# Row biases of a graph network: added by GpSimd and VectorE in place of a bf16 product on TensorE

## The chip, the cores and the metric

The kernel runs on one core of a Trainium2 chip. Its engines are TensorE (called PE in the profile, with PEld for the loading of its stationary operand), VectorE (DVE), ScalarE (ACT), GpSimd (POOL) and SyncE (SP), which only issues transfers here. The metric is the device time of one execution in microseconds (us).

## The reference, cut to what matters

Four layers of a graph network act on `x`, 512 rows of 768 numbers. Each layer normalizes `x`, gives it to a graph part and to a mixer, adds both to `x`, normalizes again and adds a feed-forward part. What matters here are the biases that are one row long, that is, one number per column, the same for all 512 rows:

```python
# layer 0, graph part, at its end: attention
qkv = nodes @ Wqkv.T + bqkv
...
attended = attn @ Wo.T + bo
return nodes + attended
# layer 0, mixer: values with a bias, and a projection with a bias
qkv = x @ qkv_w.T + qkv_b
...
out = out @ proj_w.T + proj_b
# layer 1, mixer: projection with a bias, then gamma, beta and a norm
# layers 2 and 3, mixers
out = out @ w_proj + b_proj
```

The kernel knows them as seven rows: `m0_bv` and `g0_bv` (the third of the qkv biases that belongs to the values, of mixer 0 and of the attention of graph part 0), `g0_bo` (that attention's output), and `m0_bp`, `m1_bp`, `m2_bp`, `m3_bp` (the projections of mixers 0 to 3). All matrix products are in float32, and the biases have to arrive in float32 precision too.

## The kernel before, in words

The 512 rows are `NT` = 4 tiles of `P` = 128 partitions, the 768 columns are `KC` = 6 chunks of 128 for a contraction, or two halves of `HW` = 384 for an output. The residual `self.x` ([128, 4, 768]) stays in SBUF for the whole program. Weights are streamed by SP in blocks of 1152 KB into a ring of six buffers, in the order in which the program uses them.

`tm` (L368) computes an output with rows on partitions: for each half `nb` and each row tile `t` it takes a PSUM bank, accumulates six (or twelve) products into it by `acc`, and hands the bank to `done`, which evicts it. One call is eight accumulations. `add_x` (L476) is the eviction that adds a bank to `self.x` on VectorE. `copy` (L280 and L282) is one that copies, on VectorE and ScalarE in turn.

A row bias is one more product at the end of an accumulation. `bias` (L312) fetches the row to one partition (`row`), and `parts` cuts it into three bf16 numbers that sum to the float32 value, by three copies and two subtractions on that one partition; they land at partitions 0, 32 and 64 of `self.bias3`, whose other partitions stay zero. The stationary operand is `spread(0)`, a column of `self.sel` broadcast to 128 columns, with ones at those partitions, so that a 96x128 by 96x384 product in bf16 adds the row to all 128 rows of the bank. `self.bias3` has two slots that `self.which` alternates.

The seven places, in the order of the program:

- `mix0`: the values' eight accumulations, with `m0_bv`, whose row is prepared at the program's start inside `meanwhile` by ScalarE and VectorE (all the others are prepared by GpSimd).
- `in_units`: the projection of mixer 0, cut into eight units that a generator hands out one at a time as filler inside the graph part, with `m0_bp`.
- `attention0`: its values with `g0_bv`, and `g0_wo` with `g0_bo`.
- `mix1_end`: a transfer brings `be` to 128 partitions, GpSimd adds it to `x` (L1572); then the projection with `m1_bp` is added by `put_y` onto `y`, the normalized input, which is normalized again, scaled and added to `x`.
- `project`, called by `mix2`: the projection with `m2_bp`. Mixer 2 begins with `operands` (L1861 on ScalarE, L1870 on GpSimd), which splits its input in parts, while `thirds` (L1890, L1891 on VectorE) does so with a weight.
- `last_two`: mixer 3 and the graph part of layer 3 run in alternation; each `m3_wp` accumulation has `m3_bp`, prepared behind `self.picked`.

The order on each engine is made by a list scheduler when the program is built: an engine takes, among the instructions that are ready in its model, the one that comes first in the program, so later work can move ahead of earlier work that isn't ready. `tc.issue_after(i)` adds an edge: what is issued in its block comes after `i`. At run time each engine, and the transfers that it issues, keeps its order: what stands in front and waits holds up what is behind it. GpSimd issues all the small transfers.

Of the kernel before, what the change touches and what calls it, by code (L numbers as in the profile page):

```python
# [10 lines left out]
F32 = mybir.dt.float32  # L11
# [184 lines left out]
class Net:  # L196
    def __init__(self, ctx, tc, dram, at, out):
# [28 lines left out]
        self.sel = keep.tile([96, 32], BF16, name="sel")  # L226
        self.bias3 = self.rowp.tile([96, 2, D], BF16, name="bias3", bufs=1)
        nc.gpsimd.memset(self.bias3, 0.0)
        self.which = 0

# [80 lines left out]

    def bias(self, ap, n=D, copies=None, sub=None):  # L312

        t = self.row(ap, n)
        mid = self.rowp.tile([1, D], BF16, name="mid", bufs=1)
        self.which ^= 1
        out = self.bias3[:, self.which, :n]
        self.parts(out, t[:1, :n], t[:1, :n], mid[:, :n], copies or [self.nc.gpsimd.tensor_copy] * 3,
                   sub or self.nc.gpsimd.tensor_sub)
        return out  # L320

# [45 lines left out]

    def tm(self, blocks, xT, done, bias=None, nbs=None, bias_at=0):  # L368

        for nb in range(blocks.shape[0]) if nbs is None else nbs:  # L370
            ws = [self.wk(blocks[nb, kb]) for kb in range(blocks.shape[1])]
            for t in range(NT):
                p = self.ps()
                pairs = [(xT[k][:, t * P : (t + 1) * P], ws[k // KC][:, k % KC, :]) for k in range(len(xT))]
                if bias is not None:
                    o = nb * HW - bias_at
                    pairs.append((self.spread(0), bias[:, o : o + HW]))
                self.acc(p[:, :HW], pairs)
                done(t, nb, p[:, :HW])
# [388 lines left out]
    def mix0(self, xnT, checked, held, bv):  # L768
# [3 lines left out]
        with ExitStack() as outer, ExitStack() as c:  # L772
# [12 lines left out]
            def put_v(t, nb, p):  # L785
                h = (nb - 4) * 4
                self.copy(v[:, t, h : h + 4, :96], p.rearrange("p (h d) -> p h d", h=4))

            self.tm(d["m0_wqkv"], xs, put_v, bv, nbs=(4, 5), bias_at=2 * D)
            for g in range(2):  # L790
# [64 lines left out]
    def in_units(self, aT, later, first=0):  # L855

        bias = self.bias(self.d["m0_bp"])
        for n in range(first, 8):
            nb, t = divmod(n, 4)
            if n < 2 or n % 2 == 0:  # L860
                w = self.wk(self.d["m0_wp"][nb, 0])
            p = self.ps()
            i = self.acc(p[:, :HW], [(aT[:, k, t * P : (t + 1) * P], w[:, k, :]) for k in range(KC)]
                         + [(self.spread(0), bias[:, nb * HW : (nb + 1) * HW])])
            self.add_x(t, nb, p[:, :HW])
            aT = later
            yield i.ins
# [11 lines left out]
    def project(self, c, attn, m, done=None, aT=None):  # L879

        if aT is None:
            aT = c.enter_context(self.tc.tile_pool(name=m + "_aT", bufs=1)).tile([P, KC, N], F32, name="aT")
        self.to_fm(attn, aT)
        self.tm(self.d[m + "_wp"], self.chunks(aT), done or self.add_x, self.bias(self.d[m + "_bp"]))

# [118 lines left out]
    def gnn0_any(self, nodesT, xnT, ops, EFT):  # L1004
        nc, tc, d = self.nc, self.tc, self.d
        with ExitStack() as c:
# [21 lines left out]
            with tc.tile_pool(name="g0_l", bufs=1) as lp:  # L1028
                for l in range(3):
                    h = lp.tile([P, NT, D], F32, name="h")  # L1030
                    aggT = hT = xnT
                    for f in range(KC):
                        p = self.ps()
                        self.acc(p, [(nodes[:, t, f * P : (f + 1) * P], AT[:, t, :]) for t in range(NT)])
                        nc.vector.tensor_add(aggT[:, f, :], EFP[:, f, :], p)
                    self.tm(d["g0_w1"][l], self.chunks(nodesT) + self.chunks(aggT),
                            lambda t, nb, p: self.copy(h[:, t, nb * HW : (nb + 1) * HW], p),
                            self.bias(d["g0_b1"][l : l + 1]))
# [12 lines left out]

    def attention0(self, nodesT, bv):
        nc, tc, d = self.nc, self.tc, self.d
        ns = self.chunks(nodesT)
        with ExitStack() as c:
            att = c.enter_context(tc.tile_pool(name="g0_att", bufs=1))
            two = c.enter_context(tc.tile_pool(name="g0_two", bufs=2))
            with tc.issue_after(self.after):
# [3 lines left out]
            aT = att.tile([P, KC, N], F32, name="aT")  # L1062
            self.tm(d["g0_wqkv"], ns, lambda t, nb, p: self.copy(v[:, t, (nb - 4) * HW : (nb - 3) * HW], p),
                    bv, nbs=(4, 5), bias_at=2 * D)
            for g in range(2):
# [3 lines left out]
                for h in range(4):  # L1069
# [23 lines left out]
                    else:  # L1093
                        for i in range(3):
                            self.copy(aT[96:, 3 * g + i, :], p[32 * i : 32 * i + 32])
            self.tm(d["g0_wo"], self.chunks(aT), self.add_x, self.bias(d["g0_bo"]))

    def moe(self, f, act, xn, xnT, wg, bs=None, fill=None, later=None, known=False):
# [6 lines left out]
        with ExitStack() as c:  # L1105
# [144 lines left out]
            def second_bias(t, nb):  # L1250
                p = self.ps()
                self.acc(p[:, :HW], [(gT[:, t * P : (t + 1) * P], b2[:, nb * HW : (nb + 1) * HW])])
                self.add_x(t, nb, p[:, :HW])
# [311 lines left out]
    def mix1_end(self, c, y, aT):  # L1565
# [11 lines left out]

        self.tm(d["m1_wp"], self.chunks(aT), put_y, self.bias(d["m1_bp"]))
        self.norm(y, y)
# [220 lines left out]
    def mix2(self, xnT, ops):  # L1800
        nc, tc, d = self.nc, self.tc, self.d
        xs = self.chunks(xnT)
        with ExitStack() as c:
# [27 lines left out]

            self.fm3(d["m2_wqkv"], ops, put_q, (0, 1), two)

            kv = one.tile([P, KC, P + 2], F32, name="kv")
# [233 lines left out]
    def last_two(self, xn, xnT, out, V):  # L2068
# [5 lines left out]
        with ExitStack() as c:  # L2074
# [39 lines left out]
            with tc.issue_after(self.picked):  # L2114
                bias = self.bias(d["m3_bp"])
            ready = []
            for t in range(NT):
                for nb in range(2):
                    p = self.ps()[:, :HW]
                    self.acc(p, [(qk[:, 0, k, t * P : (t + 1) * P], ws[nb][:, k, :]) for k in range(KC)]  # L2120
                             + [(self.spread(0), bias[:, nb * HW : (nb + 1) * HW])])
                    self.add_x(t, nb, p)
# [390 lines left out]
def tile_net(ctx, tc, dram, at, out, only=ALL):  # L2513
# [10 lines left out]
    with ExitStack() as ck, ExitStack() as c0:  # L2524
# [7 lines left out]
        with tc.tile_pool(name="L0", bufs=1) as pool:  # L2532
# [6 lines left out]
            def meanwhile():  # L2539
                net.constants()  # L2540
                bv.append(net.bias(net.d["m0_bv"], D, net.copies, nc.vector.tensor_sub))
                for t in range(NT):
# [9 lines left out]
            ops = net.mix0(xnT, checked, c0, bv[0])  # L2552
            bv0 = net.bias(net.d["g0_bv"])
            slot = net.which
            with tc.If(net.wrong > 0) as cmp:
                net.gnn0_any(nodesT, xnT, ops, EFT)
                net.which = 1 - slot
                net.bias(net.d["g0_bv"])
            with cmp.Else():
# [65 lines left out]
```

## Time and profile before

The time is 3710.01 us, the median of three runs (3708.91 to 3713.39). The profiled execution is another run and took 3715.96 us, with a span of 3714.2 us and a mean granted clock of TensorE of 0.992.

| | before |
|---|---|
| time, median of three runs | 3710.01 us |
| profiled execution, time and span | 3715.96 us, 3714.2 us |
| TensorE busy | 3604.8 us, 97% |
| VectorE busy | 1591.9 us, 43% |
| ScalarE busy | 892.8 us, 24% |
| GpSimd busy | 489.4 us, 13% |
| bias products (stationary `sel`, 384 columns) | 56 |
| moved from and to HBM | 714.47 MB, 192 GB/s over the span |

Times in the profile are microseconds from the span's start. A line of a timeline gives the start, the length of the group, the engine, the line of the kernel, the operation, and the tiles that it writes and reads; what stands in brackets is the idle time before it and what ended that. A line of a tile's instructions gives the count, the shortest, median and longest duration in ns, and the times between which they lie. The chain that ended last is followed back from the last instruction, at each step to what released it, or to the instruction before it on its engine; its shares say which engine's work the end had to wait for.

The feed-forward part of layer 3 fills the span from about 2605 to the end. There the weights' stream takes the DMA engines: 424 GB/s in most slices of the page, against 14 to 371 before.

### The profile page before, as it was taken

What the parts mean: (1) busy time and instruction counts of PE and PEld (TensorE: products, weight loads), DVE (VectorE), ACT (ScalarE), POOL (GpSimd) and SP (SyncE); (2) the same over time, 40 slices, a digit from 0 to 9 for tenths busy, and PEclk for the clock granted to TensorE, in tenths of its full rate; (3) what the DMA queues carried; (4) which work ended last, traced back from release to release, by engine and by line L of the source; (5) the groups of instructions that cost most, each with busy time, mean ns of one, the idle gap of its engine ahead of it and who ended that gap; (6) DMA issues with size and microseconds to landing.
All of it is one profiled execution on the core that took longest, in us unless ns stands there. A gap on an engine that the chain in (4) does not pass through costs nothing.

```text
span 3714.2 us, 39788 instructions
## 1 busy us (share of the span) xinstructions
PE 3604.8 (97%) x15741; PEld 2161.0 (58%) x15741; DVE 1591.9 (43%) x3259; ACT 892.8 (24%) x1595; POOL 489.4 (13%) x534
## 2 busy tenths in 40 slices
PE   9999999999999999999999998999999999999998
PEld 6547666445566585567878785556444444444444
DVE  8227664343212573145776764377321221221211
ACT  2223432221222263122343432254100000000000
POOL 8212101102100000010221212202000000000000
PEclk9999999999999999999999998999999999999999
DMA  5202122217501213003121114612999999999998
GB/s 214 82 14 96 58 90 102 93 44 283 199 30 56 94 57 119 26 36 112 54 76 64 64 64 184 251 51 115 371 424 423 424 424 424 424 424 424 424 425 357
DMA packets 96692, 714.47 MB, mean 192 GB/s; under 512 B 11712, under 2 KB 11968, under 8 KB 26480
## 3 DMA queue, kind: packets, MB, share of 16 engines
q1 hardware_dynamic: 75744, 604.81, 40.4%
q0 software_dynamic: 16848, 95.99, 6.8%
q10 hardware_dynamic: 3904, 11.01, 0.8%
q8 instruction: 129, 2.11, 0.2%
q14 instruction: 67, 0.55, 0.0%
HBM read 689.22 MB, written 22.54 MB: 192 GB/s over the span
## 4 chain that ended last, share of the span: by engine, by line
PE 82%; DMA 6%; issue 5%; DVE 5%; ACT 1%; POOL 0%; POOLq 0%; DVEq 0%; ACTq 0%; SPq 0%
PE ps L383 45%; PE ps L2432 12%; PE ps L1952 7%; PE ps L2448 6%; PE ps L2403 3%; PE ps L404 3%; PE ps L923 2%; DMA w<-in_f_Wg_dram 2%; DMA w<-in_f_Wu_dram 2%; PE ps L1715 2%; DMA w<-in_f_Wd_dram 1%; PE ps L1696 1%; PE ps L608 1%; DVE pt L1465 1%; DVE e L1464 1%
## 5 line engine op out<-in xcount | busy, mean ns | idle before, releaser
L2432 PE MATMUL ps<-w,xg 128*64 128x384 f32 x3072 | 565.3, 489 | 6.6 <-DMA w<-in_f_Wg_dram 3.3
L2432 PEld LDWEIGHTS ps<-w,xg 128*64 128x64 f32 x3072 | 236.8, 137 | 294.2 <-issue 262.4
L2448 PE MATMUL ps<-w,hT 128*64 128x384 f32 x1536 | 320.6, 490 | 3.3 <-DMA w<-in_f_Wd_dram 1.9
L1952 PE MATMUL ps<-ops,w 128*128 128x512 f32 x1080 | 268.0, 399 | 0.5 <-DVE w L1890 0.5
L383 PE MATMUL ps<-w,xnT 128*128 128x384 f32 x756 | 253.4, 491 | 0.2 <-ACT xnT L282 0.2
L383 PE MATMUL ps<-ops,w 128*128 128x512 f32 x972 | 242.6, 394 | 0.0
L383 PE MATMUL ps<-xnT,w 128*128 128x512 f32 x540 | 236.6, 593 | 0.1
L1952 PEld LDWEIGHTS ps<-ops,w 128*128 128x128 f32 x1080 | 204.4, 190 | 50.6 <-DVE w L1890 0.9
L2448 PEld LDWEIGHTS ps<-w,hT 128*64 128x64 f32 x1536 | 133.3, 137 | 163.2 <-issue 137.8
L2435 ACT ACTIVATE h<-ps 128x384 f32<-128x384 f32 x64 | 31.5, 492 | 794.4 <-PE ps L2432 794.4
L476 DVE TENSOR_TENSOR x<-x,ps 128x384 f32<-128x384 f32 x232 | 127.2, 553 | 199.6 <-PE ps L383 190.4
L383 PEld LDWEIGHTS ps<-ops,w 128*128 128x128 f32 x972 | 182.4, 188 | 42.5 <-issue 0.5
L383 PEld LDWEIGHTS ps<-w,xnT 128*128 128x128 f32 x756 | 144.0, 192 | 100.3 <-issue 6.8
L1861 ACT ACTIVATE w<-w 128x768 fp32r<-128x768 f32 x138 | 116.4, 847 | 331.5 <-PE ps L383 262.7
L2436 DVE TENSOR_TENSOR h<-h,ps 128x384 f32<-128x384 f32 x64 | 35.5, 554 | 354.6 <-PE ps L2432 345.9
L383 PE MATMUL ps<-w,hT 128*128 128x384 f32 x552 | 184.6, 490 | 2.9 <-ACTq L1341 1.6
L1870 POOL TENSOR_TENSOR low<-low,ops 128x512 f32<-128x512 f32 x90 | 118.5, 1317 | 432.0 <-ACT ops L1861 432.0
L383 PEld LDWEIGHTS ps<-xnT,w 128*128 128x128 f32 x540 | 101.9, 190 | 122.6 <-issue 119.3
L383 PEld LDWEIGHTS ps<-w,hT 128*128 128x128 f32 x552 | 103.1, 190 | 80.4 <-ACT xbT L282 7.1
L1890 DVE TENSOR_TENSOR w<-w,w 128x768 fp32r<-128x768 f32 x138 | 132.6, 963 | 20.4 <-ACT w L1861 20.0
L1891 DVE SCALAR_TENSOR_TENSOR w<-w 128x768 fp32r<-128x768 f32 x138 | 136.6, 992 | 2.5
L2403 PE MATMUL ps<-xnT,sw 128*128 128x512 f32 x288 | 135.4, 603 | 0.0
(566 smaller groups left out, 5155.3 us busy)
## 6 DMA issues: line engine op xcount, KB each, us to landing
w<-in_f_Wg_dram SPq DMA_DIRECT2D x128, 1152.0 KB, 22.3
w<-in_f_Wu_dram SPq DMA_DIRECT2D x128, 1152.0 KB, 22.6
w<-in_f_Wd_dram SPq DMA_DIRECT2D x128, 1152.0 KB, 22.5
w<-in_g_w_dram SPq DMA_DIRECT2D x54, 1152.0 KB, 5.1
w<-in_m_wqkv_dram SPq DMA_DIRECT2D x24, 1152.0 KB, 7.1
w<-in_g_t_dram SPq DMA_DIRECT2D x12, 1152.0 KB, 5.1
w<-in_m_wp_dram SPq DMA_DIRECT2D x11, 1152.0 KB, 5.1
ea<-in_attr_dram SPq DMA_DIRECT2D x17, 512.0 KB, 4.7
```

The costliest lines, as they stand in the source:

```text
L383: i = self.nc.tensor.matmul(out, a, b, start=n == 0, stop=n == len(pairs) - 1)
L404: return self.nc.tensor.transpose(out, in_, self.ident[:k, :k])
L476: self.nc.vector.tensor_add(xs, xs, p)
L923: nc.tensor.matmul(p, w[:, i, k], ops[:, i, k, :], start=i + k == 0, stop=i + k == KC)
L1861: return self.nc.scalar.activation(top, x, AF.Copy, scale=CUT).ins
L1870: nc.gpsimd.tensor_sub(low, v, ops[:, 0, k, :].bitcast(F32))
L1890: nc.vector.tensor_sub(low, w, top.bitcast(F32))
L1891: self.sliced_last = nc.vector.scalar_tensor_tensor(dif, low.bitcast(F32), -TIMES, top.bitcast(F32), OP.mult, OP.add).ins
L1952: nc.tensor.matmul(outs[o], w[:, i, k], ops[:, i, k, :], start=n == 0 and i + k == 0, stop=n == 4 and i + k == KC)
L2403: i = nc.tensor.matmul(p, w[:, k, :], xnT[:, k, :], start=k == 0, stop=k == KC - 1)
L2432: nc.tensor.matmul(p[a * 64 : a * 64 + 64, :HW], xg[:, k, a * CAP : (a + 1) * CAP], ws[b][a][:, k, :], start=k == 0, stop=k == KC - 1)
L2448: nc.tensor.matmul(po[nb][a * 64 : a * 64 + 64, :HW], hT[:, f * P + a * 64 : f * P + a * 64 + 64], wd[a][:, f, nb * HW : (nb + 1) * HW], s ...
```

## The change

No product for a bias is left on TensorE. A new helper, `wide`, brings a row to all 128 partitions in float32 (one buffer, so a new row waits until the last one has been read). `add_rows` does that for each of its names and then lets GpSimd add the row to the four tiles of its target, 128x768 each.

- The values of mixer 0 and of the attention are evicted by VectorE alone, by an add of the PSUM bank and the wide row, where a copy alternated between VectorE and ScalarE.
- `m0_bp` and `g0_bo` are added to `x` in `mix0`, behind `self.after` (a transfer that GpSimd issues for the edge counts), that is, long before their projections.
- `m1_bp` is added to `y` in `mix1_end` ahead of the projection, in the program behind the adds of `be`.
- `m2_bp` is added to `x` in `mix2` behind the queries' product `fm3`.
- `m3_bp` is added to `x` in `last_two`, behind `self.picked`, where the row was prepared before.
- `bias`, `bias3` with its memset at the start, and the slots of `which` are gone. In `gnn0_any`, a branch that these inputs don't take, `g0_b1` is broadcast and added on eviction.

Cut to what runs:

```diff
-        self.bias3 = self.rowp.tile([96, 2, D], BF16, name="bias3", bufs=1)
-        nc.gpsimd.memset(self.bias3, 0.0)
-        self.which = 0
...
-    def bias(self, ap, n=D, copies=None, sub=None):
-
-        t = self.row(ap, n)
-        mid = self.rowp.tile([1, D], BF16, name="mid", bufs=1)
-        self.which ^= 1
-        out = self.bias3[:, self.which, :n]
-        self.parts(out, t[:1, :n], t[:1, :n], mid[:, :n], copies or [self.nc.gpsimd.tensor_copy] * 3,
-                   sub or self.nc.gpsimd.tensor_sub)
-        return out
+    def wide(self, ap):
+
+        t = self.rowp.tile([P, D], F32, tag="wide", name="wide", bufs=1)
+        self.nc.gpsimd.dma_start(t, bass.AP(tensor=ap.tensor, offset=ap.offset, ap=[[0, P], [1, D]]))
+        return t
+
+    def add_rows(self, to, *names):
+
+        for n in names:
+            b = self.wide(self.d[n])
+            for t in range(NT):
+                self.nc.gpsimd.tensor_add(to[:, t, :], to[:, t, :], b)
...
     # tm
-                if bias is not None:
-                    o = nb * HW - bias_at
-                    pairs.append((self.spread(0), bias[:, o : o + HW]))
...
     # mix0
-                self.copy(v[:, t, h : h + 4, :96], p.rearrange("p (h d) -> p h d", h=4))
-
-            self.tm(d["m0_wqkv"], xs, put_v, bv, nbs=(4, 5), bias_at=2 * D)
+                nc.vector.tensor_add(v[:, t, h : h + 4, :96], p.rearrange("p (h d) -> p h d", h=4),
+                                     bv[:, h * 96 : (h + 4) * 96].rearrange("p (h d) -> p h d", h=4))
+
+            self.tm(d["m0_wqkv"], xs, put_v, nbs=(4, 5))
+            with tc.issue_after(self.after):
+                self.add_rows(self.x, "m0_bp", "g0_bo")
...
     # in_units
-        bias = self.bias(self.d["m0_bp"])
...
-            i = self.acc(p[:, :HW], [(aT[:, k, t * P : (t + 1) * P], w[:, k, :]) for k in range(KC)]
-                         + [(self.spread(0), bias[:, nb * HW : (nb + 1) * HW])])
+            i = self.acc(p[:, :HW], [(aT[:, k, t * P : (t + 1) * P], w[:, k, :]) for k in range(KC)])
...
     # project
-        self.tm(self.d[m + "_wp"], self.chunks(aT), done or self.add_x, self.bias(self.d[m + "_bp"]))
+        self.tm(self.d[m + "_wp"], self.chunks(aT), done or self.add_x)
...
     # attention0
-            self.tm(d["g0_wqkv"], ns, lambda t, nb, p: self.copy(v[:, t, (nb - 4) * HW : (nb - 3) * HW], p),
-                    bv, nbs=(4, 5), bias_at=2 * D)
+            self.tm(d["g0_wqkv"], ns, lambda t, nb, p: nc.vector.tensor_add(
+                v[:, t, (nb - 4) * HW : (nb - 3) * HW], p, bv[:, (nb - 4) * HW : (nb - 3) * HW]), nbs=(4, 5))
...
-            self.tm(d["g0_wo"], self.chunks(aT), self.add_x, self.bias(d["g0_bo"]))
+            self.tm(d["g0_wo"], self.chunks(aT), self.add_x)
...
     # mix1_end
-        self.tm(d["m1_wp"], self.chunks(aT), put_y, self.bias(d["m1_bp"]))
+        self.add_rows(y, "m1_bp")
+        self.tm(d["m1_wp"], self.chunks(aT), put_y)
...
     # mix2
             self.fm3(d["m2_wqkv"], ops, put_q, (0, 1), two)
+            self.add_rows(self.x, "m2_bp")
...
     # last_two
-                bias = self.bias(d["m3_bp"])
+                self.add_rows(self.x, "m3_bp")
...
-            self.acc(p, [(qk[:, 0, k, t * P : (t + 1) * P], ws[nb][:, k, :]) for k in range(KC)]
-                             + [(self.spread(0), bias[:, nb * HW : (nb + 1) * HW])])
+            self.acc(p, [(qk[:, 0, k, t * P : (t + 1) * P], ws[nb][:, k, :]) for k in range(KC)])
...
     # tile_net
-                bv.append(net.bias(net.d["m0_bv"], D, net.copies, nc.vector.tensor_sub))
+                bv.append(net.wide(net.d["m0_bv"]))
...
-            bv0 = net.bias(net.d["g0_bv"])
+            bv0 = net.wide(net.d["g0_bv"])
```

More of the change, by code (lines that the diff above doesn't have):

```diff
@@ L366, in fm3, with tm @@
                 done(nb * 3 + f, p, rest)
-    def tm(self, blocks, xT, done, bias=None, nbs=None, bias_at=0):
+    def tm(self, blocks, xT, done, nbs=None):
         for nb in range(blocks.shape[0]) if nbs is None else nbs:
@@ L373, in tm @@
                 p = self.ps()
-                pairs = [(xT[k][:, t * P : (t + 1) * P], ws[k // KC][:, k % KC, :]) for k in range(len(xT))]
-                if bias is not None:
-                    o = nb * HW - bias_at
-                    pairs.append((self.spread(0), bias[:, o : o + HW]))
-                self.acc(p[:, :HW], pairs)
+                self.acc(p[:, :HW], [(xT[k][:, t * P : (t + 1) * P], ws[k // KC][:, k % KC, :]) for k in range(len(xT))])
                 done(t, nb, p[:, :HW])
@@ L1030, in gnn0_any @@
                     h = lp.tile([P, NT, D], F32, name="h")
+                    b1 = self.bcast(lp, d["g0_b1"][l : l + 1], "b1")
                     aggT = hT = xnT
@@ L1036, in gnn0_any @@
                     self.tm(d["g0_w1"][l], self.chunks(nodesT) + self.chunks(aggT),
-                            lambda t, nb, p: self.copy(h[:, t, nb * HW : (nb + 1) * HW], p),
-                            self.bias(d["g0_b1"][l : l + 1]))
+                            lambda t, nb, p: nc.vector.tensor_add(h[:, t, nb * HW : (nb + 1) * HW], p,
+                                                                  b1[:, nb * HW : (nb + 1) * HW]))
                     self.norm(h, h)
@@ L1251, in second_bias @@
                 p = self.ps()
-                self.acc(p[:, :HW], [(gT[:, t * P : (t + 1) * P], b2[:, nb * HW : (nb + 1) * HW])])
+                self.acc(p[:, :HW], [(gT[:, t * P : (t + 1) * P], b2[:8, nb * HW : (nb + 1) * HW])])
                 self.add_x(t, nb, p[:, :HW])
@@ L2552, in tile_net @@
             ops = net.mix0(xnT, checked, c0, bv[0])
-            bv0 = net.bias(net.d["g0_bv"])
-            slot = net.which
+            bv0 = net.wide(net.d["g0_bv"])
             with tc.If(net.wrong > 0) as cmp:
                 net.gnn0_any(nodesT, xnT, ops, EFT)
-                net.which = 1 - slot
-                net.bias(net.d["g0_bv"])
             with cmp.Else():
```

## The prediction, made before the result was known

> **What bounds the kernel now.** I read the busy shares first, then the chain that ended last, then the instructions that the diff touches, and last the stretches of the timeline around each place where bias work goes or comes. The busy shares and the chain:
>
> ```profile
> PE 3604.8 (97%) x15741; PEld 2161.0 (58%) x15741; DVE 1591.9 (43%) x3259; ACT 892.8 (24%) x1595; POOL 489.4 (13%) x534
> PE 82%; DMA 6%; issue 5%; DVE 5%; ACT 1%; POOL 0%; POOLq 0%; DVEq 0%; ACTq 0%; SPq 0%
> ```
>
> TensorE (PE) is busy 97% of the span and carries 82% of the chain; GpSimd (POOL) is busy 13% and is not in the chain. So a matmul that goes away from a stage that PE binds is time gained, and POOL work costs only where it stands in front of something that PE soon waits for. The bias products are easy to find, because `sel` is the stationary operand of them alone among the 384-wide ones:
>
> ```profile
> L383 PEld LDWEIGHTS <-sel x137: 95/98/153, 84.1 to 2598.2; 96*128 96x128 bf16 x137
> L383 PE MATMUL ps<-bias,sel x56: 327/328/328, 84.4 to 2598.5; 96*128 96x384 bf16 x56
> ```
>
> There are 56 (seven rows by 8 accumulations) at 0.328 us each by their records. That is not what they cost, since matmuls overlap. The timeline of mixer 1 shows it. First eight accumulations with a bias product (the projection), then eight of the same shape without one (its values):
>
> ```profile
> 1184.16 4.03 PE L383 MATMUL ps<-w,aT 128*128 128x384 f32 x12
> 1187.71 0.10 PEld L383 LDWEIGHTS <-sel 96*128 96x128 bf16 x1
> 1188.03 0.33 PE L383 MATMUL ps<-bias,sel 96*128 96x384 bf16 x1
> 1188.19 4.03 PE L383 MATMUL ps<-w,aT 128*128 128x384 f32 x12
> ...
> 993.69 0.56 DVE L280 COPY v<-ps 128x384 f32<-128x384 f32 x1 [8.14 <-PE ps L383]
> 997.56 0.48 ACT L282 COPY v<-ps 128x384 f32<-128x384 f32 x1 [7.21 <-PE ps L383]
> 1001.43 0.56 DVE L280 COPY v<-ps 128x384 f32<-128x384 f32 x1 [7.18 <-PE ps L383]
> ```
>
> With the product an accumulation starts every 1188.19 - 1184.16 = 4.03 us (the next starts at 1192.23, so 4.035 on the mean); without it, evictions follow each other by 997.56 - 993.69 = 3.87. The product costs 0.165 us, half its record. All 56 are worth 56 x 0.165 = 9.2 us, 0.25% of the time. The measurement tells about 0.2% (7.4 us) from no change, so the whole prize is hardly above that.
>
> **Part by part, what goes.** Where PE is the bound, each row's eight products give 8 x 0.165 = 1.32 us. That holds for the values and the output projection of attention 0, the projections of mixers 1 and 2, and the end of mixer 3: 5 x 1.32 = 6.6 us.
>
> The values of mixer 0 are another matter. Their eight accumulations fill all eight PSUM banks, and PE then waits for the first bank, which it gets only after VectorE's copies:
>
> ```profile
> 111.92 1.02 DVE L280 COPY v<-ps 128x384 f32<-128x384 f32 x2 [1.86 <-ACT S L567]
> 112.70 0.33 PE L383 MATMUL ps<-bias,sel 96*128 96x384 bf16 x1
> 112.87 15.61 PE L383 MATMUL ps<-xnT,w 128*128 128x512 f32 x36
> ```
>
> The values tile is freed by the last readers of the edge counts, which the products do not touch. I take 0.3 of the 1.3.
>
> The eight projection units of mixer 0 are filler inside GNN 0. One stands on PE's path alone (0.165), one is hidden by a wait on VectorE (0), and three pairs stand where PE and VectorE arrive almost together (h is ready at 389.19, PE at 389.42), so 0.2 to 0.33 a pair: 0.9 in all.
>
> The preparation of a row into three bf16 parts is five instructions on one partition, 0.81 + 1.63 + 0.81 + 1.64 + 0.82 = 5.7 us. Six rows have it on POOL, where it ends long before its products and is hidden (0). The first row, `m0_bv`, has it on VectorE and ScalarE; VectorE's two subtractions (1.03 and 1.01 us, at 44.3 and 46.4) lie just ahead of the stretch 49 to 64, where VectorE paces PE with some 2 us of PE idle. Bounds 0 and 2; I take 1.5, because PE's wait there is as long as the work removed. The memset of `bias3` (1.41 us at the start of POOL) is hidden by the first load, which lands at 7.22: 0. Sum of what goes: 6.6 + 0.3 + 0.9 + 1.5 = 9.3 us.
>
> **What is added.** POOL gets 20 adds of 128x768 (five rows by four row tiles). Mixer 1 has that same instruction already, with its own transfer:
>
> ```profile
> 986.28 7.11 POOL L1572 TENSOR_TENSOR x<-x,be 128x768 f32<-128x768 f32 x4 [6.18 <-DMA be<-in_m_be_dram]
> ```
>
> That is 1.80 us an add, 7.2 a row: 36 us in all against 6 x 5.7 = 34 removed, so POOL's load stays. Each row's transfer grows from 3 KB to 384 KB, as with `be`, which lands 6.7 us after issue against 3.2. The `wide` buffer is single, so a transfer waits for the last row's adds; the rows are hundreds of us apart except `m0_bp` and `g0_bo`. These two run one after the other (some 2 x (7.2 + 6.7) = 28 us) where POOL is idle from 126.9 to 264.7: 0. The sixteen value evictions become VectorE adds from PSUM; the nearest row (the residual add from PSUM) is 0.553 us against 0.56 for the copy, and at one per 3.87 us they stay hidden: 0. The half that leaves ScalarE gives 0, as PE waits for neither there.
>
> The remaining 12 adds (mixers 1, 2, 3) become ready while a norm makes its `xn`, just when VectorE and POOL are about to feed PE again. Two prices are in dispute. The first is what a POOL add does to VectorE work beside it. Mixer 3 has such a pair:
>
> ```profile
> L2111 POOL TENSOR_TENSOR qk<-qk x6: 1653/1712/1722, 2508.2 to 2517.2; 128x512 f32<-128x512 f32 x6
> ...
> L2110 DVE SCALAR_TENSOR_TENSOR qk<-qk,f x6: 739/1748/1761, 2507.4 to 2514.3; 128x512 f32<-128x512 f32 x6
> ```
>
> Alone the VectorE instruction takes 0.74 us, beside POOL's 1.75: +1.0 at 512 wide, which scaled to 768 I estimate at +1.4 for an add. VectorE instructions that read PSUM are not stretched (0.56 beside POOL's adds of `y` to `x` at the end of mixer 1).
>
> [...]
>
> The second price is POOL's own order: an add in front of a POOL instruction or transfer that PE needs. Place by place:
>
> Mixer 1: the adds onto `y` become ready at 978 to 984, beside a few VectorE instructions on the norm's statistics (0.16 us each). Bounds 0 and 1.7 (one blocked for nearly an add); I take 0.8, the middle, since no row shows these at the same moment. The four adds of `be` follow on POOL and move some 7 us later, with POOL idle until 1176: 0.
>
> Mixer 2: its chain is tight.
>
> ```profile
> 1588.32 1.85 DVE L471 TENSOR_SCALAR xn<-x,mv,rs 128x768 f32<-128x768 f32 x3
> 1590.56 0.94 DVE L1890 TENSOR_TENSOR w<-w,w 128x768 fp32r<-128x768 f32 x1
> 1591.53 0.95 DVE L1891 SCALAR_TENSOR_TENSOR w<-w 128x768 fp32r<-128x768 f32 x1
> 1592.60 0.68 DVE L471 TENSOR_SCALAR xn<-x,mv,rs 128x768 f32<-128x768 f32 x1
> 1593.33 0.88 PE L404 MATMUL ps<-ident,xn 128*128 128x128 f32 x6 [2.04 <-DVE xn L471]
> 1595.93 8.75 POOL L1870 TENSOR_TENSOR low<-xnT,ops 128x512 f32<-128x512 f32 x6 [44.13 <-ACT ops L1861]
> ```
>
> PE waits 2.04 us for the last `xn`, and POOL is idle until 1595.93. An add can start when its `xn` is made, from about 1589, and would then lie beside L1890, L1891 and the last `xn`. Ends: 0 (adds put after L1870's six) and 4 x 1.4 = 5.6 (every add collides); three adds fit before 1593.3, 4.2; I take 2.8, two collisions. A gain is excluded, since the place loses nothing but its products.
>
> Mixer 3: POOL issues the mask and two small weight loads there (at 2395.23, 2398.82 and 2401.08, landing about 2403.6, when PE uses them at 2403.69), and tiles of `x` become ready at 2392.0 to 2399.6. Ends 0 and 7.2 (four adds ahead of the loads); after 2402 POOL is free for 80 us. I take 1.2: one add ahead of the first, less the slack in which it was idle. Sum of the losses: 0.8 + 2.8 + 1.2 = 4.8.
>
> The last stage (2605 to the end) is bound by its transfers, at 0.99 of the DMA engines; its stream starts when PE releases the first ring buffer, so earlier gains move its start and stay. The profiled run took 3715.96 us (span 3714.2) and would take 3715.96 - 9.3 + 4.8 = 3711.5. It lies 6.0 above the median of the runs, so the median becomes 3710.0 - 4.5 = 3705.5.
>
> **Rivals.** (A) The adds fall into POOL's idle time and meet nothing: losses 0, 3710.0 - 9.3 = 3700.7. For it: POOL is idle after each of these places for tens of us, and the row of `be` shows no harm. Against: the adds are ready in the tight stretch, and this program moves later work ahead of earlier where an engine is free (a memset that stands behind L1870 in the program ran 44 us before it).
>
> (B) Slower: each of the 12 exposed adds stalls the chain for its whole length, as the VectorE instruction of L2110 was stalled for nearly all of L2111. 12 x 1.8 = 21.6, less 9.3: 3710.0 + 12.3 = 3722.3. It breaks even at 9.3 / 12 = 0.78 us an add and passes the 0.2% at (9.3 + 7.4) / 12 = 1.39, which is just the scaled row. Against: in mixers 1 and 3 most VectorE work at that moment reads PSUM or is 0.16 us long.
>
> (C) Nothing comes of it: the products leave but PE waits as long for something else (the next weight, an eviction by VectorE alone, a reordered queue), 3710. For it: the values of mixer 0, where that happens. Against: the clean 4.03 against 3.87 in mixer 1.
>
> **How the numbers follow.** The sum as forecast 0.38, A 0.30, B 0.17, C 0.15. The forecast's own range is 3702 to 3709, from the terms' bounds. Faster by over 0.2% means below 3702.6: most of A (0.27) and the lower part of the forecast (0.09), 0.36. Slower means above 3717.4: B nearly whole and a little of C, 0.18. The rest is 0.46. The range, 3697 to 3719, reaches past A by the 3.7 us to which the runs themselves spread, and to an add price of 1.5 us in B.
>
> **What would show it.** The 56 products are gone, and the projection of mixer 1 has a pitch of 3.87. POOL shows twenty new adds of 128x768 at 1.8 (up to 2.5 would mean that they collide). In mixer 2, right: PE's wait for the last `xn` grows from 2.04 to about 5; A: it stays at 2; B: over 7. In mixer 3, right: PE waits for `bd` by about 1 us more. Wrong would be a sum of the stretches 0 to 2605 that changes by more than the 9.3 of the products or by a changed order of queues far from these places, which nothing in the profile lets me price.

## The result and the profile after

The changed kernel takes 3722.58 us, the median of eight runs (3718.72 to 3726.83); the kernel before, in eight runs beside them, 3710.84 (3707.07 to 3713.61). The ratio is 1.0033, with an interval of 1.0024 to 1.0042: slower by 12 us. The forecast was 3705.5, with a range of 3697 to 3719.

The profiled execution of the changed kernel took 3726.83 us, with a span of 3724.8. First the page's line of busy time, and two of its groups of instructions. What stands behind the second bar is the idle time ahead of the group and what ended it:

```profile
PE 3601.9 (97%) x15680; PEld 2161.2 (58%) x15685; DVE 1608.4 (43%) x3265; ACT 887.8 (24%) x1584; POOL 489.0 (13%) x523
...
L379 PE MATMUL ps<-xnT,w 128*128 128x512 f32 x540 | 242.2, 604 | 5.5 <-DVE v L783 5.5
```

The products are gone, POOL is as busy as it was (489), and the busy times hardly tell that anything happened. One group does: TensorE waited 5.5 us for an eviction of mixer 0's values.

That the products cost what was said is seen in mixer 1's projection, whose evictions now come every 1192.07 - 1188.20 = 3.87 us, against a pitch of 4.03 before (the timeline, VectorE alone):

```profile
1188.20 0.56 DVE L1574 TENSOR_TENSOR xn<-xn,ps 128x384 f32<-128x384 f32 x1 [2.73 <-PE ps L379]
...
1192.07 0.55 DVE L1574 TENSOR_TENSOR xn<-xn,ps 128x384 f32<-128x384 f32 x1 [2.72 <-PE ps L379]
...
1195.94 0.55 DVE L1574 TENSOR_TENSOR xn<-xn,ps 128x384 f32<-128x384 f32 x1 [2.72 <-PE ps L379]
```

So something takes back the gain and 12 us more. Laying each of TensorE's instructions beside its twin in the trace of before gives four places where the changed kernel falls behind.

**Mixer 1** (timeline of the kernel before, then of the changed one):

```profile
980.02 0.16 DVE L1369 SCALAR_TENSOR_TENSOR mv<-mv,rs 128x1 f32<-128x1 f32 x1
981.39 0.87 PE L404 MATMUL ps<-ident,xn 128*128 128x128 f32 x6 [0.95 <-ACT xn L1378]
```

```profile
979.76 3.62 POOL L320 TENSOR_TENSOR xn<-xn,wide 128x768 f32<-128x768 f32 x2
979.96 3.45 DVE L1367 SCALAR_TENSOR_TENSOR mv<-mv,rs 128x1 f32<-128x1 f32 x1
984.52 1.54 PE L400 MATMUL ps<-ident,xn 128*128 128x128 f32 x6 [4.15 <-ACT xn L1376]
```

A VectorE instruction on one number per partition, 0.16 us long elsewhere, takes 3.45 us beside two of the new adds. ScalarE's normalization stands behind it, and TensorE behind that: 4.15 us of wait against 0.95 before.

**Mixer 2**:

```profile
1593.37 3.35 DVE L467 TENSOR_SCALAR xn<-x,mv,rs 128x768 f32<-128x768 f32 x3
1594.13 6.73 POOL L320 TENSOR_TENSOR x<-x,wide 128x768 f32<-128x768 f32 x3 [37.84 <-DVE xn L467]
1597.12 2.09 DVE L1890 TENSOR_TENSOR w<-w,w 128x768 fp32r<-128x768 f32 x1
1599.25 2.43 DVE L1891 SCALAR_TENSOR_TENSOR w<-w 128x768 fp32r<-128x768 f32 x1
1602.53 1.54 PE L400 MATMUL ps<-ident,xn 128*128 128x128 f32 x6 [4.87 <-DVE xn L467]
```

Three adds run from 1594.1 on; the three normalizations take 3.35 where they took 1.85, L1890 2.09 for 0.94, L1891 2.43 for 0.95, and TensorE waits 4.87 for the last tile where it waited 2.04. From the first of these transposes to the last it falls from 5.05 us behind (1594.19 against 1589.14) to 9.20 (1602.53 against 1593.33): 4.2 us. The lengths of the single normalizations (count, then shortest, median and longest in ns) show that one of them alone is held, and it has only one tensor among its inputs (`x`; `mv` and `rs` are one number per partition):

```profile
L467 DVE TENSOR_SCALAR xn<-x,mv,rs x4: 673/678/2175, 1593.4 to 1601.8; 128x768 f32<-128x768 f32 x4
```

**Mixer 3**: the adds do not run at the expert part's end at all, but at 2556, amid the graph part's head loop:

```profile
2556.07 8.86 POOL L320 TENSOR_TENSOR x<-x,wide 128x768 f32<-128x768 f32 x4 [0.96 <-DVE x L2221]
2556.52 2.30 DVE L1462 TENSOR_TENSOR e<-e,e 128x512 f32<-128x512 f32 x1
...
2558.86 2.19 DVE L1463 SCALAR_TENSOR_TENSOR pt<-e,C 128x512 f32<-128x512 f32 x1
```

Four VectorE instructions in a row take 2.2 to 2.3 us in place of 0.69. The releaser says why so late: the add to `x` waited for L2221, where the graph part adds its own heads to `x` and stands ahead of it in the program.

**Mixer 0**: here no add runs. Before, and then after, the load of the first projection weight (SP), the transfer of S (POOL), and ScalarE's step that waits for S to land:

```profile
95.80 0.56 POOL L585 DMA_DIRECT2D S<-S  x1 [0.30 <-POOL S L580]
96.75 0.33 SPq L289 DMA_DIRECT2D w<-in_m_wp_dram  x1
100.98 1.47 ACT L567 CAST S<-whole 128x1536 f32<-128x1536 uint8 x1 [7.02 <-DMA S<-S]
```

```profile
95.03 0.33 SPq L286 DMA_DIRECT2D w<-in_m_wp_dram  x1
95.24 0.56 POOL L581 DMA_DIRECT2D S<-S  x1 [0.30 <-POOL S L576]
104.39 1.47 ACT L563 CAST S<-whole 128x1536 f32<-128x1536 uint8 x1 [10.99 <-DMA S<-S]
115.33 1.02 DVE L783 TENSOR_TENSOR v<-ps,wide 128x384 f32<-128x384 f32 x2 [1.86 <-ACT S L563]
115.94 4.64 PE L379 MATMUL ps<-xnT,w 128*128 128x512 f32 x5 [5.46 <-DVE v L783]
```

TensorE is some 2 us earlier, so it frees a ring buffer earlier, and SP sends 1152 KB off 0.2 us ahead of S where it went 1 us behind it. S lands 9.2 us after its issue (95.24 to 104.39) in place of 5.2. The counts' chain is 3.4 us late, the values' tile is freed that much later, and TensorE waits 5.46 us.

Then comes a second price. The table of stretches has, behind the stretch and its length, each engine's busy time, and the granted clock as the third number from the end. Mixer 0 at 116 to 122, mixer 1 and mixer 2, before and then after:

```profile
116.00:122.00 6.00, 6.00 (x16) 2.65 (x15) 1.50 (x2) 0.63 (x1) 2.68 (x7) 1.00 0.44 175
976.00:986.00 10.00, 7.11 (x37) 4.78 (x36) 7.39 (x22) 5.70 (x11) 2.82 (x6) 0.89 0.88 329
1588.00:1606.00 18.00, 14.64 (x55) 9.29 (x56) 13.95 (x20) 11.12 (x19) 9.25 (x7) 0.91 0.01 1
```

```profile
116.00:122.00 6.00, 6.00 (x8) 2.58 (x9) 3.91 (x10) 0.00 (x0) 5.03 (x11) 0.53 0.35 122
976.00:986.00 10.00, 4.72 (x27) 3.31 (x25) 8.73 (x18) 3.93 (x8) 6.93 (x10) 0.79 0.99 365
1588.00:1606.00 18.00, 10.72 (x44) 6.96 (x43) 14.26 (x20) 4.34 (x9) 9.29 (x5) 0.82 0.00 1
```

Behind each long wait the granted clock is lower than in the kernel before (0.53 against 1.00, 0.79 against 0.89, 0.82 against 0.91): after 115.94 it is "busy" all 6 us and gets through 8 matmuls where it did 16. The mean granted clock of the span is 0.989 against 0.992; 0.011 x 3725 - 0.008 x 3714 = some 11 us of full clock more are withheld by this estimate (not all of it while TensorE had work).

The clock is lowest, 0.53, behind the wait of 5.46 us. But a wait as long as that is not needed: before, with waits of up to 1.00 and 2.04 us there, mixers 1 and 2 have 0.89 and 0.91, and e4_quiet (below), whose wait in mixer 1 is 0.95 us, has 0.79 in that stretch like the changed kernel.

### The profile page after: what moved, and what is told of

Same layout as the page of the kernel before. It is cut to its first block, busy times and chain, and to the rows that moved or that the text cites. A ratio compares the mean times of both kernels' runs of the same rounds, so it can differ in the third digit from the quotient of the medians.

```text
span 3724.8 us, 39662 instructions
## 1 busy us (share of the span) xinstructions
PE 3601.9 (97%) x15680; PEld 2161.2 (58%) x15685; DVE 1608.4 (43%) x3265; ACT 887.8 (24%) x1584; POOL 489.0 (13%) x523
## 5 line engine op out<-in xcount | busy, mean ns | idle before, releaser
L1890 DVE TENSOR_TENSOR w<-w,w 128x768 fp32r<-128x768 f32 x138 | 132.5, 962 | 19.1 <-ACT w L1861 18.7
L1891 DVE SCALAR_TENSOR_TENSOR w<-w 128x768 fp32r<-128x768 f32 x138 | 138.1, 1003 | 2.5
```

The lines of the kernel that those rows point to most:

```text
L1890: nc.vector.tensor_sub(low, w, top.bitcast(F32))
L1891: self.sliced_last = nc.vector.scalar_tensor_tensor(dif, low.bitcast(F32), -TIMES, top.bitcast(F32), OP.mult, OP.add).ins
```

## The experiments

Times below stand beside runs of the kernel before on the same chip, in four groups: 3709.91 us (27 runs) for the first four kernels, 3712.0 (17) for b_again, b_five, e5_one_input and e7_m2, 3711.21 (22) for e8_m3, e9_gate and e10_none_gate, 3712.4 (15) for b_gate. The ratios and their intervals are those on record; they are not the quotients of the medians.

**What the products were worth, taken away alone: nothing that can be told.** Without any of the seven rows, and then with VectorE's eviction of the values but without the adds:

```diff
# e1_none and e2_no_adds
-        for n in names:
-            b = self.wide(self.d[n])
-            for t in range(NT):
-                self.nc.gpsimd.tensor_add(to[:, t, :], to[:, t, :], b)
+        pass
...
# e1_none alone (so too in attention0)
-                nc.vector.tensor_add(v[:, t, h : h + 4, :96], p.rearrange("p (h d) -> p h d", h=4),
-                                     bv[:, h * 96 : (h + 4) * 96].rearrange("p (h d) -> p h d", h=4))
+                self.copy(v[:, t, h : h + 4, :96], p.rearrange("p (h d) -> p h d", h=4))
```

> The changed kernel without any of the seven bias rows: no product on TensorE, no add by GpSimd, no broadcast of a row, and the values evicted by alternating copies as before (all seven row biases are left out of the result). It bounds what the products were worth. Theory: only products in stages that TensorE paces to the end count. Those of mixer 0 (values and units) and the start do not, because in the trace of before and of after TensorE waits for the same weight at 305 us (5.6 us idle until 305.6 in after, 7.8 until 305.5 in before); so 5 rows x 1.32 = 6.6 us, 3704 against a before of 3710.8. Rival: all 56 products at 0.165 plus the start, 9.2 + 1.5 = 10.7 us, 3700. Second rival, the products were hidden: within 2 us of before.

> The changed kernel without GpSimd's twenty adds and their five broadcasts; the values are still evicted by VectorE with their bias (the five projection biases are left out). Theory: the loss is the adds, so this is at e1_none, 3704, give or take 2, even if TensorE waits some 5 us for the values of mixer 0, since that is absorbed by 305 us. Rival, the eviction by VectorE alone is what costs (5.1 us of wait at 113 to 116 us and 2.9 us at half clock behind it in the trace of after): 3704 + 8 = 3712, and the adds then cost about 10 of the 18 us between 3704 and 3722.

Measured: e1_none 3707.24 us (ratio 0.9998, 0.9989 to 1.0007), e2_no_adds 3708.7 (0.9999, 0.9989 to 1.0008). The two agree, so the eviction by VectorE alone costs nothing that can be told. But both are level with before: taken alone the removal of all the bias work gave, by the interval, something between 4 us less and 3 us more, and the smallest sum of products was 6.6. The wait in mixer 0 is in both traces, 5.37 us for a copy in e1_none and 5.14 in e2_no_adds, so neither adds nor evictions make it.

**The changed kernel once more, and with its adds in quiet places:**

> The changed kernel once more, beside the others on one chip. Every theory: 3722, 11 to 12 us over before. Its trace tells which of the losses seen in the first one come again: theory says the waits of TensorE for the normalized tiles in mixer 1 (4.2 us, 1.0 before) and mixer 2 (4.9, 2.0 before) come again, and those that hang on the moment of a transfer or of a halved clock (mixer 0 at 116 us, mixer 3 at 2470) may not.

```diff
# e4_quiet: mixer 1 (last is the last add of be)
-        self.add_rows(y, "m1_bp")
+        with self.tc.issue_after(last):
+            self.add_rows(y, "m1_bp")
...
# mixer 2: from behind fm3 to behind L1870's last subtraction
             self.operands(ops, lambda k: (xnT[:, k, :], self.rest(), None))
+            with tc.issue_after(self.low_last):
+                self.add_rows(self.x, "m2_bp")
...
# mixer 3: from behind fm to behind the graph part's setup
             next(beside)
+            with tc.issue_after(self.rows_set):
+                self.add_rows(self.x, "m3_bp")
```

> The changed kernel with twelve of the adds put elsewhere on GpSimd's queue and nothing else changed: those of mixer 1 behind the adds of be, those of mixer 2 behind the six subtractions of L1870, those of mixer 3 ahead of the graph part's head loop, behind the last memset of its setup. Theory, the adds cost only by stopping VectorE instructions that TensorE waits for: all of the loss goes, 3704 to 3706, and the waits for the normalized tiles fall back to 1.0 and 2.0 us. Rival, twenty adds and their transfers of 384 KB cost wherever they lie: over 3715.

Measured: e3_after 3723.97 us (1.0040, 1.0027 to 1.0054), e4_quiet 3710.28 (1.0006, 0.9997 to 1.0015). So 13.7 us of the loss (by the ratios 12.6, give or take 6) are twelve adds in the wrong place, the same number of adds costing next to nothing in another; e3_after less e2_no_adds gives 15.3. In e3_after the waits come again (4.16 in mixer 1, 4.87 in mixer 2, and 5.34 in mixer 0, which by the expectation might have been chance). In e4_quiet those of mixers 1 and 2 are back at 0.95 and 2.04:

```profile
982.11 1.54 PE L400 MATMUL ps<-ident,xn 128*128 128x128 f32 x6 [0.95 <-ACT xn L1376]
...
1591.52 0.87 PE L400 MATMUL ps<-ident,xn 128*128 128x128 f32 x6 [2.04 <-DVE xn L467]
```

Still, the level is 3710, not the 3704 to 3706 expected: what e1_none lacks is lacking here too.

**A second profile of before, and the price of a product in the other direction:**

> The kernel before once more, for a second profile of it. Its first profiled execution took 3716, 6 us over its median; theory: at its median of 3710 the second one stands 3 to 6 us earlier by the end of the feed-forward part of layer 2 (where the first waited 3.45 us for a gather at 2390 that the trace of e1_none does not show), and otherwise the same. Rival: the two traces agree within 1 us up to 2600, and the difference lies in the last stage, which the transfers bind.

```diff
# b_five, in tm, in_units and last_two
-                    pairs.append((self.spread(0), bias[:, o : o + HW]))
+                    pairs += [(self.spread(0), bias[:, o : o + HW])] * 5
```

> The kernel before with each bias product issued five times in its accumulation (224 more products; the bias is counted five times in the result). It measures the price of a product in the direction that can't be hidden by a transfer that comes too late. By the pitch of mixer 1, 0.165 us each: 224 x 0.165 = 37 us if all are on the path (3747); 5 rows of 8, 4 x 6.6 = 26 us, if mixer 0 absorbs its own (3736). Rival, the products are hidden nearly everywhere, as the 1 to 3 us between e1_none and before would have it: 3714 to 3722.

b_again took 3711.39 us in its profiled execution (span 3709.6). It differs from the first trace of before in two places. One is the wait at 2390, as expected, some 3.4 us. The other was not expected, a granted clock of 0.62 in place of 1.00 in mixer 0; the same stretch in the first trace and then in the second:

```profile
225.00:234.00 9.00, 8.22 (x19) 5.03 (x19) 1.38 (x2) 3.54 (x6) 0.00 (x0) 0.62 0.00 0
```

```profile
225.00:234.00 9.00, 7.29 (x31) 4.37 (x28) 1.80 (x3) 3.76 (x7) 0.00 (x0) 1.00 0.00 0
```

From 205 us to there TensorE's longest wait is 0.78 us in both traces (at 225.92 in the first), so what lowered the clock in one of them stays open. The first trace of before was 0.7 us ahead of b_again until there and is 2.7 behind from there on, which hid that the changed kernel is late in mixer 0. Against b_again, e1_none comes to 113 us 3.3 us ahead, is 4.7 behind at 116, and still 2.9 behind at 310: the weight at 305 does not absorb it, which had been the theory of these expectations. The 5.6 and 7.8 us of idle time that they name there are ScalarE's, which waits for that weight; TensorE is busy all the time from 290 to 310 us in both traces.

b_five took 3775.75 us (1.0169, 1.0156 to 1.0183), more than either expectation. The trace tells why: the biases counted five times send the rows to other experts, two expert blocks more run (20 gathers of `xb` for 18), and between 2088 and 2377 us it loses 27 us by that. Up to 2088 it is 26.6 us behind, for six rows with 6 x 8 x 4 = 192 more products, that is 0.139 each, and in mixer 3's eight accumulations another 5.2, or 0.163 each. So most of a product's 0.165 us reaches the path nearly everywhere. (Some 5 us more are lost between 2377 and 2550, which this does not explain.)

**How VectorE is held beside the adds.**

```diff
# e5_one_input, in the norm at the end of the expert parts
-                turn(V.scalar_tensor_tensor, mv[:, 0:1], mv[:, 0:1], -1.0, r, OP.mult, OP.mult)
+                turn(V.tensor_scalar, mv[:, 0:1], mv[:, 0:1], r, -1.0, OP.mult, OP.mult)
```

> The changed kernel with the adds where they are; in the norm at the end of the expert parts the 128x1 VectorE instruction that multiplies mv by -1 and by rs takes rs as a scalar operand (one tensor input) in place of a second tensor input. In the trace of after it took 3.45 us beside two adds of mixer 1 in place of 0.16. Theory, an instruction with two tensor inputs in SBUF is kept out while GpSimd adds run: it takes 0.16 to 0.2 us again, TensorE's wait in mixer 1 falls from 4.2 to 1.0, 3722 - 3.5 = 3719. Rival, VectorE is held by a semaphore or by any use of SBUF beside the adds: it still takes over 3 us, 3722.

> The changed kernel with only mixer 2's adds put behind the six subtractions of L1870. Theory: TensorE's wait for the last normalized tile falls from 4.9 to 2.0 us, the 1.3 us wait for the third goes too, and with the halved clock behind it 4.5 to 5.5 us come back: 3717. Rival, the adds cost nothing there and the waits are chance: 3722.

> The changed kernel with only mixer 3's adds moved, to the end of the graph part's setup. Theory: VectorE's instructions L1462 and L1463 take 0.69 us again in place of 2.2 to 2.3 (four of them beside the adds at 2556 in after), and the 2.8 us that TensorE lost there come back: 3719. Rival, there is slack behind them: 3722.

e5_one_input: 3717.73 us (1.0019, 1.0010 to 1.0029), where the changed kernel had 1.0033 and 1.0040. The adds start as close ahead of the 128x1 instruction as in the changed kernel (0.26 us, there 0.20) and run as long, and it is no longer held; the transposes come 1.63 us behind the start of the adds, where it was 4.76:

```profile
983.45 3.62 POOL L320 TENSOR_TENSOR xn<-xn,wide 128x768 f32<-128x768 f32 x2
983.52 0.16 DVE L1367 RECIPROCAL rs<-rs 128x1 f32<-128x1 f32 x1
983.71 0.21 DVE L1367 TENSOR_SCALAR mv<-mv,rs 128x1 f32<-128x1 f32 x1
983.84 1.01 DVE L1367 BATCH_NORM_STATS2 st<-x 128x6 f32<-128x384 f32 x2
...
985.08 0.87 PE L400 MATMUL ps<-ident,xn 128*128 128x128 f32 x6 [0.96 <-ACT xn L1376]
```

That excludes a semaphore, and any use of SBUF as such: reciprocal, one-input product and statistics (0.16, 0.21 and 1.01 us) are in the middle of the adds as long as in the turn ahead of them in this trace (0.16, 0.22 and 1.01, from 981.14 us on). For this instruction it is the second tensor input that is kept out (3.45 us with it, 0.21 without). It is not the only case: the 128x768 normalization of mixer 2, with one tensor input, was held too (2.18 in place of 0.68).

This profiled execution took 3723.82 us, 6 over the median of its kernel. Beside the trace of the changed kernel it gains 2.6 us between 979 and 990 and has a span shorter by 3.1; the 5 to 8 us that come back by the ratios are known to some 4 us only.

e7_m2: 3718.29 us (1.0022, 1.0011 to 1.0032), and the wait in mixer 2 is 2.04 again. e8_m3: 3721.5 us (1.0030, 1.0020 to 1.0040), within the uncertainty of the changed kernel's own; its trace has L1462 and L1463 at 0.68 to 0.69 again, so the stretching there is the adds', but by the times no more than 1 to 4 us come back. Beside the trace of the changed kernel its own gains 2.8 us between 2550 and 2600, as expected, and keeps them to the end; that is one execution of each.

How long the 128x1 instruction was held, the changed kernel's trace shows: its 3.45 us end at 983.41, with the second of the two adds (983.38). Why the 128x768 normalization is held, no run here shows.

**The collision in mixer 0.** One wait more: the first projection weight behind the last transfer of S. It is tried on e4_quiet, on e1_none, and on the kernel before.

```diff
# e9_gate, e10_none_gate, b_gate, in mix0
+            self.gate, self.before = self.after, 0
             with tc.issue_after(self.after):
                 self.rest_of_mix = self.in_units(aT, xnT)
```

> e4_quiet with one wait more: the first weight of mixer 0's projection is loaded only when GpSimd's last transfer of S (self.after) has landed. In the traces of after, e1_none and e4_quiet that load, set off by a TensorE that is 2 us earlier, starts ahead of the transfer of S at 95 us, S lands 3 to 4 us later, TensorE waits 5.5 us for the first values' bank and then has half its clock for 6.8 us; in the kernel before the load starts behind S. Theory: without that collision the wait is under 1 us, and of the 8 us lost there, of which 3 to 6 reach the end (by the second trace of before, mixer 0 ends 2.9 us later in e1_none although it began 2.8 earlier), 3 to 5 come back: 3705 to 3707, faster than before by 3 to 5 us. Rival, all of it is absorbed at 305 us by the weight of the graph part: 3710 as e4_quiet.

> e1_none (all seven row biases left out) with the same wait: what the products were worth when the earlier TensorE runs into nothing. Theory: 0.165 us for each of the 40 in stages that TensorE paces, and a part of the rest, 7 to 9 us under before, 3702 to 3704. Rival, the products' time is lost in many small places: 3707 as e1_none.

> The kernel before, with the wait of e9_gate and nothing else: the first weight of mixer 0's projection behind the last transfer of S. It tells whether the gain of e9_gate is the wait's own. Theory: in the kernel before the load starts behind S anyway (at 96.8 to 97.4 against 95.8), so nothing is gained, 3710 to 3711, and the gain of e9_gate is the products'. Rival: the wait alone gives 3 us or more, 3707 or less, since the load takes part of the transfer rate from S also there.

| kernel | us | ratio to before | interval |
|---|---|---|---|
| e9_gate: the change, adds in quiet places, the wait | 3702.45 | 0.9980 | 0.9971 to 0.9989 |
| e10_none_gate: no bias work, the wait | 3699.56 | 0.9971 | 0.9960 to 0.9981 |
| b_gate: the kernel before, the wait | 3711.4 | 1.0001 | 0.9992 to 1.0010 |

The wait gains nothing that can be told for the kernel before. With it the change is faster than before by 9 us (4 to 11 by the interval), more than the 3 to 5 expected, and the removal of the bias work is worth 11.6 us (7 to 15 by the interval), where without the wait no gain could be told. The traces show where: between 113 and 130 us e9_gate gains 7.6 us on e4_quiet, and e10_none_gate 7.5 on e1_none. The spans of these profiled executions differ by 4.8 and 2.8 us only, part of the gain being lost in mixer 1, where the clock is lower in the two with the wait (960 to 1080: 0.96 in both, against 0.97 in e4_quiet and 1.00 in e1_none). The timeline of e9_gate has S landing 4.2 us after its issue, and TensorE's wait gone:

```profile
94.62 0.56 POOL L581 DMA_DIRECT2D S<-S  x1 [0.30 <-POOL S L576]
98.86 1.47 ACT L563 CAST S<-whole 128x1536 f32<-128x1536 uint8 x1 [6.07 <-DMA S<-S]
...
110.41 14.00 PE L379 MATMUL ps<-xnT,w 128*128 128x512 f32 x32 [0.67 <-DVE v L783]
...
118.96 0.33 SPq L286 DMA_DIRECT2D w<-in_m_wp_dram  x1
```

The wait costs nothing of its own: the weight, now loaded at 119, is first used in the projection's first unit, which ran at 268 in the trace of before.

## Why the prediction was wrong

It forecast 5 us less and 12 us more were measured. Two steps failed: the collision in mixer 0, put at nothing, and the price of the twelve adds, put at 4.8 us where 13.7 to 15.3 were measured. Term by term:

- *The bias product costs 0.165 us and is on the path in five places.* Right: the pitch is 3.87, mixer 3 shows 0.163 for an added product, and what goes is worth 11.6 us once nothing collides (9.3 forecast, inside the interval). In place, e1_none and e4_quiet gain 0.3 us on b_again at each of the three pairs of units, as forecast.
- *The start: 1.5, as long as the work removed.* Too much: between 50 and 80 us these two traces gain 0.7 us on b_again.
- *The values of mixer 0: 0.3 us gained, because the tile is freed by the counts, "which the products do not touch".* This step failed. They touch it by way of a transfer: an earlier TensorE sends the next weight off ahead of S. By e9_gate against e4_quiet (0.9980 and 1.0006) this costs some 9 us (7.6 in the traces): in the changed kernel's trace a wait of 5.46 us and a granted clock of 0.53 in 116 to 122 us behind it. The prediction followed what TensorE waits for, and did not ask what it sets off when it is earlier, though it had noted that for the last stage.
- *Mixer 2: 2.8, at most 5.6.* The mechanism was right, and the sign that was named for it came (a wait of about 5: 4.87); the size was inside the bounds in the trace, 4.2, with three collisions for two, and is 4 to 7 in the time by e7_m2.
- *Mixer 1: 0.8, at most 1.7, one instruction blocked for one add.* The right instruction, but the bound was wrong: it was held for the rest of two adds, 3.45 us, and 5 to 8 us came back in e5_one_input by the ratios, 2.6 in place in its trace. The row of mixer 3 that the price came from (1.75 for 0.74) shows VectorE getting in after each of GpSimd's instructions (the first slowed one ended at 2510.40, 0.54 us behind GpSimd's at 2509.86).
- *Mixer 3: 1.2, adds ahead of small loads at 2395.* Wrong in place and mechanism. The adds could not start there: an earlier write to `x` in the program order holds them until 2556, where they stretch VectorE work (2.2 to 2.3 us for 0.69). e8_m3 puts the price at 1 to 4 us by the times, 2.8 in the traces.
- *The adds of `m0_bp` and `g0_bo`, VectorE's evictions, the memset: 0.* For the adds and the evictions, right within the some 3 us that e1_none, e2_no_adds and e4_quiet differ by at most; no run takes the memset alone.

Rival B named the number, 3722.3, by luck, and half of the cause. Adds that stall the chain were the larger loss, 13.7 to 15.3 us, or about 1.2 us for each of the twelve, not 1.8; and the gain of 9.3 that it subtracted had been lost elsewhere. By these runs the sum is -11.6, + 9 for the collision, + 13.7 to 15.3 for the adds: 11 to 13 us, against 12 measured (which they must nearly give, being differences of the same few runs).

The lower clock (0.53 behind the wait in mixer 0) was in no term of the sum. What is left open is the split of the adds' loss. By the times the single prices (5 to 8, 4 to 7, 1 to 4) have uncertainties of 3 to 4 us each. In place, between the starts of the same matmuls, the changed kernel's trace loses on that of e4_quiet 2.0 us in mixer 1 (975 to 990), 3.9 in mixer 2 (1590 to 1612) and 2.8 in mixer 3 (2556 to 2600), and e3_after's 1.8, 4.1 and 4.4. The rest lies where no add runs, much of it where the granted clock is lower: 0.66 against 1.00 of e4_quiet in 1056 to 1066 (3.3 us from 990 to 1075), 0.72 against 1.00 in 2468 to 2480. Whether the adds bring these about is not shown.

## What to carry to other kernels

In this case an add moved to an idle GpSimd was free only where VectorE did nothing that TensorE waits for soon and that the add holds up: here a 128x1 instruction with two tensor inputs in SBUF (3.45 us for 0.16), one of 128x768 with two (2.09 for 0.94), and a 128x768 normalization with one (2.18 for 0.68). Queued behind such a stretch the same adds cost next to nothing (3710.28 us, with 3709.91 before); a small operand given to VectorE as a scalar freed the 128x1 instruction (0.21 us). When work goes from the engine that binds, list the transfers that its progress sets off and look what they will now overtake: here one ordering edge on a weight turned a gain of nothing into 9 us. Where each wait is a few us, compare two traces of the kernel before first, since a lower clock in one execution, as at 225 us here (0.62 against 1.00), can hide the very place that changed.

## What the runs showed of the hardware

- One VectorE instruction on 128x1 numbers took 3.45 us with two tensor inputs in SBUF while GpSimd added; with the second one as a scalar it took 0.21 beside the same adds, and two statistics of 384 columns took 1.01 there, as they did ahead of the adds. A 128x768 normalization, one tensor input and two numbers per partition, took 2.18 beside an add, and 0.68 alone.
- Two transfers issued 0.2 us apart on two queues: the one behind, S, landed 9.2 us after its issue, against 5.2 when it went 1 us ahead of the other and 4.2 with the other held back.
- A wait of 5.46 us was followed by a granted TensorE clock of 0.53 in 116 to 122 us. A clock of 0.62 also came in one of two traces of the same kernel behind waits of at most 0.78 us, and 1.00 in the other. Over the span the mean granted clock is 0.989 to 0.992 in the eight runs of the changed kernel, 0.991 to 0.995 in the runs of before beside the experiments.
